# Four graph layers in float32: moving one group of tail products, and projecting a 32-column tile in four column tiles

## The chip, the cores and the metric

The kernel runs on one core of one Trainium2 chip. The metric is the device time of one execution in microseconds; the time given for a kernel is the median of its runs. A core has TensorE (PE, matrix products; its weight loads are listed as PEld), VectorE (DVE), ScalarE (ACT), GpSimd (POOL) and SyncE (SP). POOL and SP here issue DMA transfers and do nearly no computing. Each engine works through its own instructions strictly in order: an instruction that waits holds all that stand behind it on that engine.

## What is computed

Four graph layers on 2708 nodes with 512 features, on one 2708 x 2708 adjacency matrix. Each layer normalizes, aggregates over the graph, projects, and adds to `x`. Layers 0 to 2 differ in scaling, bias and self loops; layer 3 has a gated graph convolution beside an attention over the edges:

```python
h = relu(layernorm(x)); x = x + relu(aug @ h @ W0)            # layer 0, aug = D^-1/2 (A + I) D^-1/2
h = relu(layernorm(x)); x = x + (a_norm @ h @ W1.T + b1)      # layer 1
h = relu(layernorm(x)); x = x + relu(A_norm @ h @ W2)         # layer 2, with self loops
h = relu(layernorm(x))                                        # layer 3
x_a = attn @ (h @ W_sa); x_b = adj @ (h @ W_gcnb) + b_gcnb
x = x + sigmoid(attn_a * x_a + attn_b * x_b)                  # gates from type sums and h
```

## The kernel before

**Tiles.** The nodes are cut into four quarters of 677. Each quarter gives five tiles of 128 nodes (`KT = 5`, 20 in all), and 37 nodes are left over. Their first 32, of all four quarters together, make tile 20 (`NF`). The last 5 of each quarter, padded to 8, make 4 x 8 = 32 nodes for tile 21 (`NF + 1`); its 32 columns are repeated four times to fill 128 partitions. A matrix column block of one quarter is handled in two pieces (`U = 2`) of 339 columns.

**Aggregation.** The product of the 20 full tiles with the adjacency matrix is done by a two-level seven-product scheme: `OUTER` lists seven outer products, and each is done, for each piece `u`, by seven inner products of five accumulating matmuls (`product`, L506). `inner_x` and `inner_y` (L454, L471) build the sums of operands on DVE: `inner_y` makes `t1`, `t2`, `t4` and `t3` (L480 to L484), of 1695 elements a partition each; `add_loops` (L425, L431) adds multiples of the identity. `multiply` (L515) issues the inner products in a fixed order into banks `pa`, `pb`, `pa`, `pc`, `pd`, `pc`, `pd`; between them ScalarE copies `pa` (L543), DVE forms `u2` and `u3` (L549, L556), and `give` (L521, L525 to L534) adds results into `agg`. All of these and the tail products below take banks in turn from a pool of five PSUM buffers (`ps_agg`), with two more in `ps_out`.

**Tail products.** What tiles 20 and 21 contribute is added by `tail_products` (L567): for a quarter `q` and a piece, four matmuls with tile 20's 128 rows (L571), then four with 32 rows of tile 21 each, on the four row groups of the array (L576). `tails` (L603) runs them for a list of quarters and adds the four banks to `agg` (L621). `tail_rows` (L580) loads the rows they multiply and adds the self loops to them (L600).

**Layer 0 around the change.** `first_aggregate` (L662) is written out by hand because it also builds the degrees, and operand sums are kept for later layers in DRAM. Buffers are tight there: the tail rows of quarter 1 go into `own_t3`, which held `t3` of the products before, so they can be loaded only after product four's second piece has read it. The order is: product four's last piece, the tail products of quarters 0 and 1 (L849), then product five in two pieces (L857 to L864). Product five's second piece multiplies blocks `t1[1]`, which come by a load (L708) and an accumulating DMA (L712). `tc.issue_after(ins)` puts what it encloses behind `ins` on the engine of `ins`; where nothing says so, a scheduler decides the order of instructions on each engine when the program is built. `at_end` is the list of the additions into `agg` so far.

**The projection.** After the aggregation of a half, each tile's four column blocks of `agg` (`tile_cols`, L163) are the stationary operands of four matmuls, accumulated in one bank, with a weight matrix moving (`project`, L877, used in `next_x`; layer 3's gates in `gated`, L1016, with 257 columns; the attention's output in `attention`, L1114, with 512 or 256). For the tail tiles `tile_cols` gathers the columns into a scratch row by four copies (L174); for tile 21 `repeat` (L157, L160) doubles them twice to 128. Scratch rows come from `new_y`, which hands out two places in turn.

Of the kernel before, what the change touches and what calls it, by code (L numbers as in the profile page):

```python
# [8 lines left out]
FP = mybir.dt.float32  # L9
# [3 lines left out]
P = 128  # L13
D = 512
NC = D // P
N = 2708
NQ = 4
# [4 lines left out]
U = 2  # L22
W = (Q + 1) // U
NF = NQ * KT
NT = NF + 2
R1P = 8
G = NQ * R1P
# [10 lines left out]
def gnn_kernel(  # L38
# [20 lines left out]
    nc = tc.nc  # L59

    const = ctx.enter_context(tc.tile_pool(name="const", bufs=1))
# [11 lines left out]

    ident = const.tile([P, P], FP, name="ident")
    make_identity(nc, ident)
    again_ident = const.tile([P, G], FP, name="again_ident")
    nc.vector.tensor_add(again_ident, ident[:, 0:G], ident[:, G : 2 * G])
    for k in range(2, P // G):
        nc.vector.tensor_add(again_ident, again_ident, ident[:, k * G : (k + 1) * G])
    ones = const.tile([P, P], FP, name="ones")  # L80
    nc.vector.memset(ones, 1.0)
    first = const.tile([P, 32], FP, name="first")
# [43 lines left out]
    own_t3 = block(ends, 3 * BLK)  # L126
# [18 lines left out]
    def new_y():  # L145
        return take(y_places)
# [10 lines left out]
    def repeat(g, n):  # L157

        while n < P:
            nc.vector.tensor_copy(g[..., n : 2 * n], g[..., 0:n])  # L160
            n *= 2

    def tile_cols(a, t):  # L163

        cs = [a[:, f, :, c] for f in range(a.shape[1]) for c in range(a.shape[3])]
        if t < NF:
            q = t // KT
            return [full_cols(c[:, q // 2, q % 2], t) for c in cs]
        o, m = (KT * P, R0) if t == NF else (KT * P + R0 - PAD, R1P)
        if a.shape[5] == R0 + R1:  # L170
            o -= KT * P
        g = new_y().rearrange("p (c n) -> p c n", c=NC)
        for c, src in enumerate(cs):
            nc.vector.tensor_copy(  # L174
                g[:, c, 0 : NQ * m].rearrange("p (i q r) -> p i q r", i=2, q=2),
                src[:, :, :, o : o + m],
            )
        repeat(g[:, 0 : len(cs)], NQ * m)
        return [g[:, c] for c in range(len(cs))]


    def small_cols(tag, n):
# [320 lines left out]
    def bank(name):  # L503
        return ps_agg.tile([P, W], FP, tag="agg", name=name)
# [75 lines left out]
    def tail_rows(self_loops, q, pieces=None):  # L580


        blk = None
        if pieces is None:
            blk = free.pop(0)
            both = blk[:, 0 : 2 * U].rearrange("p (s u) w -> p s u w", s=2)
            pieces = [both[:, :, u] for u in range(U)]
            for s in range(2):
                nc.sync.dma_start(both[:, s], yt[s, :, q])
        else:  # L590
            for u in range(U):
                load_tails(q, u, pieces[u])
        if self_loops:
            o = (KT * P) % W
            for s, i, c0, n in (
                (0, ident[:, q * R0 : (q + 1) * R0], o, R0),
                (1, again_ident[:, q * R1P + PAD : (q + 1) * R1P], o + R0, R1),
            ):
                d = pieces[U - 1][:, s, c0 : c0 + n]
                nc.vector.tensor_add(d, d, i)  # L600
        return blk, pieces
# [60 lines left out]
    def first_aggregate(epilogue):  # L662
# [180 lines left out]
                    )  # L843
        for k, y in ((0, y22[0]), (1, y22[1]), (2, y22[0]), (3, y22[1])):
            minus_y22 = third_less(k, y, at_y[-1])
        own = own_t3[:, 0 : 2 * U].rearrange("p (s u) w -> p s u w", s=2)
        with tc.issue_after(minus_y22):
            rows = [early_rows, tail_rows(True, 1, [own[:, :, u] for u in range(U)])]
        tails(True, (0, 1), rows)  # L849
        t1 = [t2u, [y22[0], more[2], y22[1], t4[3]]]  # L850
        assert not free
        came = accumulated({QUAD[k]: t1[1][k] for k in (1, 0, 2, 3)}, "y12", 1, "y11")
# [4 lines left out]
        for u in range(U):  # L857
            more_loops = OUTER[5][2] - (OUTER[6][2] if u == 0 else 0)
            with tc.issue_after(came) if u == 1 else nullcontext():
                keep_all(t1[u], "t1", u, QUAD[1:3])  # L860
            with tc.issue_after(minus_y22 if u == 0 else at_end[-3]):
                ys = inner_y(t1[u], u, more_loops)
            keep_all(t1[u], "t1", u, QUAD[::3])
            multiply(xs_, ys, u, p5)  # L864
        with tc.issue_after(at_y[-1]):
            nc.vector.tensor_add(XC, XC, XA)
        free += t2u + [f for f in t1[1] if f is not more[2]]
# [7 lines left out]


    def project(w_sb, t):  # L877
        cs = tile_cols(agg, t)
        po = ps_out.tile([P, D], FP, tag="out", name="po")
        for c in range(NC):  # L880
            nc.tensor.matmul(  # L881
                po, cs[c], w_sb[:, c, :], start=(c == 0), stop=(c == NC - 1)
            )
        return po, cs

    def load_x(t, src):
        xt = take(xt_places)
# [3 lines left out]
    def next_x(ts, w_sb, scale, bias, src, colscale, after=None):  # L891
        for g in groups(ts):
            n, t0 = len(g), g[0]
            mv = small.tile([P, KT, 2], FP, tag="mv", name="mv")
            xts = []
            for s, t in enumerate(g):
                xt = load_x(t, src)
                po, _ = project(w_sb, t)
                y = new_y()
                if bias is None:  # L900
                    nc.scalar.activation(y, po, AF.Relu, scale=scale[:, t : t + 1])
                else:
                    nc.vector.scalar_tensor_tensor(
                        y, po, scale[:, t : t + 1], bias, ALU.mult, ALU.add
                    )
                nc.vector.tensor_add(xt, xt, y)  # L906
                nc.gpsimd.dma_start(xs[t], xt)  # L907
                stats(xt, mv[:, s, :])
                xts.append(xt)
            rstd = rstd_of(mv, n)  # L910
            if colscale is not None:
                nc.vector.tensor_mul(rstd[:, :n], rstd[:, :n], colscale[:, t0 : t0 + n])
            sh = shift_of(mv, rstd, n)
            for s, t in enumerate(g):
                normalized(t, xts[s], rstd[:, s : s + 1], sh[:, s : s + 1])
                if after is not None:
                    after(t)
# [5 lines left out]
    w_sb = []  # L923
# [92 lines left out]
    def gated(ts):  # L1016

        for t in ts:
            cs = tile_cols(agg, t)
            po = []  # L1020
            for k in range(2):
                pk = ps_out.tile([P, GW], FP, tag="out", name="pg")
                for c in range(NC):
                    nc.tensor.matmul(  # L1024
                        pk, cs[c], wg_sb[:, c, k, :], start=(c == 0), stop=(c == NC - 1)
                    )

                nc.scalar.activation(
                    ga[:, t, k : k + 1], pk[:, D // 2 :], AF.Tanh,
                    bias=hd[:, t, 2 + k : 3 + k], scale=0.5,  # L1030
                )
                po.append(pk)
            nc.vector.tensor_scalar(ga[:, t, :], ga[:, t, :], 0.5, 0.5, ALU.mult, ALU.add)
            y = new_y()
            for k in range(2):
                f = slice(k * (D // 2), (k + 1) * (D // 2))
                nc.vector.tensor_add(y[:, f], po[k][:, 0 : D // 2], bg_bc[:, f])
            nc.scalar.activation(y, y, AF.Copy, scale=ga[:, t, 1:2])
            nc.gpsimd.dma_start(xbs[t], y)
# [74 lines left out]
    def attention(t, columns, pieces=1):  # L1114
        xt = load_x(t, xs)
        y = load_x(t, xbs)
        nc.scalar.activation(xt, xt, AF.Copy, bias=0.5)
        sm = ps_sm.tile([P, NT], FP, tag="sm", name="pse")
        nc.tensor.matmul(sm[:, 0:1], columns(t), ones[:, 0:1], start=True, stop=True)
        cs = tile_cols(agg, t)  # L1120
        g = small.tile([P, 1], FP, tag="ge", name="ge")
        nc.vector.tensor_add(g, sm[:, 0:1], eps[:, t : t + 1])
        nc.vector.reciprocal(g, g)
        nc.vector.tensor_mul(g, g, ga[:, t, 0:1])
        n = D // pieces
        for k in range(pieces):
            f = slice(k * n, (k + 1) * n)
            pE = ps_out.tile([P, n], FP, tag="out", name="pE")
            for c in range(NC):
                nc.tensor.matmul(pE, cs[c], wsa_sb[:, c, f], start=(c == 0), stop=(c == NC - 1))  # L1130
            nc.vector.scalar_tensor_tensor(y[:, f], pE, g, y[:, f], ALU.mult, ALU.add)
            nc.scalar.activation(y[:, f], y[:, f], AF.Tanh, scale=0.5)
            nc.vector.scalar_tensor_tensor(xt[:, f], y[:, f], 0.5, xt[:, f], ALU.mult, ALU.add)
            for o, m, to in place(t):
                nc.gpsimd.dma_start(out[to : to + m, f], xt[o : o + m, f])
# [77 lines left out]
    xt_places = [a[:, k * D : (k + 1) * D] for a in flat for k in range(3)]  # L1213
    todo = [(t, lambda t, se_t=se_t: full_cols(se_t, t)) for t, se_t in todo]
    for k, t in ((1, NF + 1), (3, NF)):
        todo.insert(k, (t, lambda t: tile_cols(tail_sums, t)[0]))
    for n, (t, columns) in enumerate(todo):
        attention(t, columns, 1 if n + 1 < len(todo) else 2)

# [60 lines left out]
```

## Time and profile before

| | us |
|---|---|
| median of three runs | 2114.19 (2109.82 to 2119.08) |
| the profiled execution's own time | 2109.49 |
| its span, first to last instruction | 2107.3 |
| PE busy | 2059.4 (98%) |
| DVE busy | 1414.6 (67%) |
| ACT busy | 406.8 (19%) |
| POOL busy | 182.8 (9%) |
| projection matmuls L881, with columns from `agg` | 207.6, 480 records |
| mean granted clock of PE | 0.995 of full |

One float32 matmul appears as two records. In a group's line the first number is busy time, the second the mean duration of one record; records overlap, so a record's duration is more than its share of the time. In a timeline, a line gives start, length, engine, line of the kernel, operation, output and input; in brackets stands the idle time of the engine before it, and what ended it. In a list of waits the numbers are total, times and longest, in us. In a table by windows the columns are length, busy time of the engine, its records, the clock granted to PE, the busy share of the DMA engines, and GB/s.

### The profile page before, as it was taken

The numbers are of one execution on the slowest core, as the hardware profiler recorded it, in microseconds if no ns is written. First come the engines' busy times: TensorE is split into PE (matmuls) and PEld (weight loads), VectorE is DVE, ScalarE is ACT, GpSimd is POOL, SyncE is SP. The second block draws the span as 40 slices with busy tenths as digits, with TensorE's granted clock in tenths as the row PEclk, the third lists the DMA queues.
The fourth block names the chain that finished last, engine by engine and source line by source line (L and its number), as shares of the span: only waits on it lengthen the run. The fifth ranks groups of instructions, "written<-read, shape, count | busy, mean of one in ns | idle before, by whom it ended". The sixth has DMA issues, their size and how long they took to land.

```text
span 2107.3 us, 20074 instructions
## 1 busy us (share of the span) xinstructions
PE 2059.4 (98%) x7328; PEld 1284.3 (61%) x7328; DVE 1414.6 (67%) x2488; ACT 406.8 (19%) x827; POOL 182.8 (9%) x330
## 2 busy tenths in 40 slices
PE   5999989999999999999999999999999999999998
PEld 2666645646666555666664556666777666666665
DVE  4588867756777778766687889867537755666512
ACT  1430001130000011100002120000107533444410
POOL 0110111120000012100002120000001000000011
PEclk9999989999999999999999999999999999999999
DMA  9998594555545454655444574555451233233220
GB/s 369 300 376 272 186 314 157 192 179 180 176 159 174 138 178 138 230 170 172 165 157 161 201 240 161 182 165 171 161 177 61 93 103 112 86 103 101 90 73 26
DMA packets 79746, 360.86 MB, mean 171 GB/s; under 512 B 10668, under 2 KB 15660, under 8 KB 79520
## 3 DMA queue, kind: packets, MB, share of 16 engines
q1 hardware_dynamic: 50672, 245.43, 34.0%
q0 software_dynamic: 28976, 114.15, 16.7%
q8 instruction: 58, 0.95, 0.2%
q14 instruction: 40, 0.33, 0.0%
HBM read 294.61 MB, written 62.15 MB: 169 GB/s over the span
## 4 chain that ended last, share of the span: by engine, by line
PE 86%; DVE 6%; DMA 4%; issue 2%; POOL 1%; ACT 0%; SPq 0%; POOLq 0%; DVEq 0%; ACTq 0%
PE pe L1183 17%; PE pa L509 14%; PE pc L509 13%; PE pd L509 13%; PE po L881 9%; PE pb L509 7%; PE pE L1130 4%; PE pg L1024 3%; PE pt L571 3%; DMA obuf<-in_yb_dram 2%; PE pt L576 1%; PE pe L571 1%; DMA ends<-in_yt_dram 1%; DMA ends<-xs 1%; DVE ends L976 1%
## 5 line engine op out<-in xcount | busy, mean ns | idle before, releaser
L1183 PE MATMUL pe<-obuf,h 128*128 128x339 f32 x1280 | 372.8, 448 | 0.0
L509 PE MATMUL pa<-obuf,h 128*128 128x339 f32 x1040 | 315.8, 448 | 2.5 <-ACT h L223 1.4
L1183 PEld LDWEIGHTS pe<-obuf,h 128*128 128x128 f32 x1280 | 240.9, 189 | 126.6 <-issue 10.0
L509 PEld LDWEIGHTS pa<-obuf,h 128*128 128x128 f32 x1040 | 196.1, 189 | 106.3 <-issue 5.5
L881 PE MATMUL po<-ends,agg 128*128 128x512 f32 x480 | 207.6, 593 | 0.0
L1098 ACT ACTIVATE e<-r,nsr 128x339 f32<-128x339 f32 x352 | 170.8, 566 | 25.8 <-DVE obuf L1102 11.5
L509 PE MATMUL pc<-t,h 128*128 128x339 f32 x560 | 169.7, 449 | 2.7 <-DVE u L556 2.6
L509 PE MATMUL pb<-t,s 128*128 128x339 f32 x560 | 171.1, 452 | 1.1 <-DVE s L441 0.7
L509 PE MATMUL pd<-t,s 128*128 128x339 f32 x560 | 169.0, 448 | 0.0
L509 PE MATMUL pd<-obuf,s 128*128 128x339 f32 x550 | 166.3, 448 | 0.3 <-DVE agg L530 0.3
L543 ACT COPY v<-pa 128x339 f32<-128x339 f32 x56 | 24.7, 440 | 722.5 <-PE pa L509 719.4
L881 PEld LDWEIGHTS po<-ends,agg 128*128 128x128 f32 x480 | 90.9, 190 | 114.3 <-issue 109.3
L509 PEld LDWEIGHTS pc<-t,h 128*128 128x128 f32 x560 | 105.5, 189 | 58.7 <-DVE u L556 5.4
L509 PEld LDWEIGHTS pb<-t,s 128*128 128x128 f32 x560 | 106.4, 191 | 56.7 <-issue 1.8
L509 PEld LDWEIGHTS pd<-t,s 128*128 128x128 f32 x560 | 105.9, 189 | 54.1
L509 PEld LDWEIGHTS pd<-obuf,s 128*128 128x128 f32 x550 | 104.1, 189 | 53.8 <-DVE agg L530 1.3
L509 PE MATMUL pc<-obuf,s 128*128 128x339 f32 x450 | 136.1, 448 | 0.0
L509 PEld LDWEIGHTS pc<-obuf,s 128*128 128x128 f32 x450 | 85.1, 189 | 43.8 <-issue 0.5
L481 DVE TENSOR_TENSOR t<-obuf,t 128x1695 f32<-128x1695 f32 x55 | 105.5, 1918 | 0.0
L907 POOL DMA_DIRECT2D xs<-ends x66 | 35.9, 544 | 769.7 <-DVE ends L906 694.5
L1200 DVE COPY agg<-pe 128x339 f32<-128x339 f32 x16 | 7.5, 506 | 137.8 <-PE pe L576 137.8
L482 DVE TENSOR_TENSOR t<-obuf,t 128x1695 f32<-128x1695 f32 x52 | 99.7, 1916 | 0.1
(275 smaller groups left out, 2395.6 us busy)
## 6 DMA issues: line engine op xcount, KB each, us to landing
obuf<-in_yb_dram SPq DMA_DIRECT2D x132, 847.5 KB, 4.6
obuf<-osumt SPq DMA_DIRECT2D x100, 847.5 KB, 4.5
osumt<-obuf POOLq DMA_DIRECT2D x22, 847.5 KB, 10.3
xs<-ends POOLq DMA_DIRECT2D x66, 256.0 KB, 2.3
ends<-xs POOLq DMA_DIRECT2D x61, 256.0 KB, 3.9
obuf<-in_yt_dram SPq DMA_DIRECT2D x28, 339.0 KB, 3.6
obuf<-in_yb_dram POOLq DMA_DIRECT2D x11, 847.5 KB, 11.7
ends<-in_yb_dram SPq DMA_DIRECT2D x9, 847.5 KB, 9.0
```

The source lines that it names most:

```text
L481: nc.vector.tensor_add(t2, o22, t1)
L482: at_y.append(nc.vector.tensor_add(t4, o21, t2).ins)
L509: last = nc.tensor.matmul(ps, x[:, k, :], y[:, k, :], start=start and k == 0, stop=k == KT - 1, skip_group_check=not start,)
L543: at_v.append(nc.scalar.copy(v, pa).ins)
L571: nc.tensor.matmul(ps[c], h[:, NF, c * P : (c + 1) * P], tl[:, 0, :], start=start, stop=False)
L576: nc.tensor.matmul(ps[c], h[g, NF + 1, c * P : (c + 1) * P], tl[g, 1, :], start=False, stop=True)
L881: nc.tensor.matmul(po, cs[c], w_sb[:, c, :], start=(c == 0), stop=(c == NC - 1))
L907: nc.gpsimd.dma_start(xs[t], xt)
L1024: nc.tensor.matmul(pk, cs[c], wg_sb[:, c, k, :], start=(c == 0), stop=(c == NC - 1))
L1098: nc.scalar.activation(e[:, k], row, AF.Exp, bias=nsr[:, t, s : s + 1], scale=1.0)
L1130: nc.tensor.matmul(pE, cs[c], wsa_sb[:, c, f], start=(c == 0), stop=(c == NC - 1))
L1183: nc.tensor.matmul(pe[c], h[:, t, c * P : (c + 1) * P], a, start=(t == 0), stop=False)
```

## The change

Two edits. First, in layer 0 the tail products of quarter 1 are no longer run with those of quarter 0 ahead of product five, but between its first and second piece; the self loops on their rows are ordered behind the first piece's last `u3`. The loads of the rows carry no such order, since they are issued by SP and not by DVE. Second, for tile 21 the four column blocks are no longer repeated to 128 columns and accumulated: each 32-column block goes to a column group of its own in one bank, so the four partial results stand on the four partition groups; ScalarE copies the bank to a scratch row, and one matmul with `all_again` (128 x 128, one wherever row and column agree modulo 32) sums them and repeats the sum on all four groups. Only the attention's own column sums still use `repeat`.

```diff
-    again_ident = const.tile([P, G], FP, name="again_ident")
+    all_again = const.tile([P, P], FP, name="all_again")
+    again_ident = all_again[:, 0:G]
     nc.vector.tensor_add(again_ident, ident[:, 0:G], ident[:, G : 2 * G])
     for k in range(2, P // G):
         nc.vector.tensor_add(again_ident, again_ident, ident[:, k * G : (k + 1) * G])
+    for k in range(1, P // G):
+        nc.vector.tensor_copy(all_again[:, k * G : (k + 1) * G], again_ident)
...
-    def tile_cols(a, t):
+    def tile_cols(a, t, again=False):
...
-        repeat(g[:, 0 : len(cs)], NQ * m)
-        return [g[:, c] for c in range(len(cs))]
+        n = NQ * m
+        if again:
+            repeat(g[:, 0 : len(cs)], n)
+            n = P
+        return [g[:, c, 0:n] for c in range(len(cs))]
+
+    def tile_product(t, cs, ws):
+        n = ws[0].shape[-1]
+
+        def bank():
+            return ps_out.tile([P, n], FP, tag="out", name="po")
+
+        po = bank()
+        if t <= NF:
+            for c in range(NC):
+                nc.tensor.matmul(po, cs[c], ws[c], start=(c == 0), stop=(c == NC - 1))
+            return po
+        for c in range(NC):
+            nc.tensor.matmul(po[c * G : (c + 1) * G], cs[c], ws[c], start=True, stop=True)
+        y = new_y()[:, 0:n]
+        nc.scalar.copy(y, po)
+        po = bank()
+        nc.tensor.matmul(po, all_again, y, start=True, stop=True)
+        return po
...
-        own = own_t3[:, 0 : 2 * U].rearrange("p (s u) w -> p s u w", s=2)
-        with tc.issue_after(minus_y22):
-            rows = [early_rows, tail_rows(True, 1, [own[:, :, u] for u in range(U)])]
-        tails(True, (0, 1), rows)
+        tails(True, (0,), [early_rows])
...
             multiply(xs_, ys, u, p5)
+            if u == 0:
+                own = own_t3[:, 0 : 2 * U].rearrange("p (s u) w -> p s u w", s=2)
+                with tc.issue_after(at_u3[-1]):
+                    rows = tail_rows(True, 1, [own[:, :, v] for v in range(U)])
+                tails(True, (1,), [rows])
...
     def project(w_sb, t):
-        cs = tile_cols(agg, t)
-        po = ps_out.tile([P, D], FP, tag="out", name="po")
-        for c in range(NC):
-            nc.tensor.matmul(
-                po, cs[c], w_sb[:, c, :], start=(c == 0), stop=(c == NC - 1)
-            )
-        return po, cs
+        return tile_product(t, tile_cols(agg, t), [w_sb[:, c, :] for c in range(NC)])
```

`gated` and `attention` call `tile_product` in the same way in place of their own four matmuls.

## The prediction

> **What bounds the kernel now.** I read the page's busy table first, then the waits of TensorE, then the timeline around its longest wait inside the kernel, then the granted clock there. Busy time and waits of TensorE (PE):
>
> ```profile
> PE 2059.4 (98%) x7328; PEld 1284.3 (61%) x7328; DVE 1414.6 (67%) x2488; ACT 406.8 (19%) x827; POOL 182.8 (9%) x330
> ...
> PE dg_ps L292 <- DMA tails<-in_yt_dram: 16.8, 1, 16.8
> PE pt L571 <- DVE agg L530: 7.8, 1, 7.8
> ...
> PE pt L571 <- DVE agg L621: 2.1, 2, 1.6
> ```
>
> PE is the bound: 98% busy, and apart from the first load its one long wait is in layer 0's first tail products (L571). So a PE microsecond removed, or a PE wait removed, is a microsecond of the end, unless something else becomes late. The timeline there, PE and then VectorE (DVE):
>
> ```profile
> 268.87 0.84 PE L571 MATMUL pt<-tl,h 128*128 128x339 f32 x2
> 277.47 1.50 PE L571 MATMUL pt<-tl,h 128*128 128x339 f32 x2 [7.77 <-DVE agg L530]
> 280.61 2.63 PE L571 MATMUL pt<-tl,h 128*128 128x339 f32 x4 [1.64 <-DVE agg L621]
> ...
> 291.68 3.13 PE L509 MATMUL pa<-obuf,h 128*128 128x339 f32 x10
> ...
> 267.71 0.50 DVE L530 TENSOR_TENSOR agg<-pc,u 128x339 f32<-128x339 f32 x1
> 275.19 0.19 DVE L600 TENSOR_TENSOR ends<-ends,ident 128x32 f32<-128x32 f32 x1 [6.98 <-DMA ends<-in_yt_dram]
> ...
> 276.91 0.51 DVE L530 TENSOR_TENSOR agg<-pd,u 128x339 f32<-128x339 f32 x1
> ```
>
> The reader should see a head-of-line block. DVE stands at L600, which adds the self loops to the tail rows of quarter 1, until their DMA lands. Behind it waits L530, which would empty bank `pd`; PE's second tail matmul of the second half needs that bank. PE does not need quarter 1's rows yet. The clock, in windows of 3.413 us (columns: us, PE busy, granted clock, DMA share, GB/s):
>
> ```profile
> 268.68:272.09 3.41, 1.02 (x6) 1.00 1.03 416
> 272.09:275.50 3.41, 0.00 (x0) 0.50 1.04 364
> ...
> 282.33:285.74 3.41, 3.41 (x12) 0.50 1.07 227
> 285.74:289.16 3.42, 3.42 (x18) 1.00 1.03 212
> ```
>
> The wait also costs half clock from 272.1 to 285.7. DMA is full throughout.
>
> For the second edit I read 32-column matmuls (the column sums, L292) and one tail-tile projection (L881):
>
> ```profile
> 110.39:113.94 3.55, 3.55 (x48) 1.00 1.01 414
> 454.57:458.01 3.44, 3.44 (x10) 1.00 0.30 123
> ```
>
> 46 records (the window's count includes two neighbours) of 339 columns with 32-column weights take 3.55 us: a float32 matmul is two records, a full-width record takes 0.286 us (ten in 2.86), so 46 in a row would be 13.2. Four run side by side. Eight full 512-column records take 3.44.
>
> **What the Trainium skill says.** "TensorE: Matmul & The Clock Gate", Part 1, has the clock drop to half after an idle window and return after a busy one, in a free-running 3413 ns window; the trace fits, from 272.09 to 285.74 being four of them. "TensorEngine Tiling (Array Packing)", Key Properties: column tiles load and multiply in parallel, and a change of tiling mode drains the array. The trace agrees with both; entering costs about 0.1 us and leaving 0.1 (12 groups of 0.286 are 3.43 of the 3.55). "DMA: Bandwidth & Descriptors", Issuing engines are not separate DMA queues: loads from SP and POOL share the same 16 engines. Here they are at a share of 0.98 from 255 to 312 us.
>
> **The change, part by part.** Sums are against the profiled execution, 2109.49 us (span 2107.3), which is 4.7 below the median of 2114.19.
>
> Setup: three more 128x32 copies on DVE, 0.2 us each by L174's like, while PE waits 16.8 us for its first load: 0; exposed they would be 0.6.
>
> Layer 0's tails. L600 leaves this place. In the built order DVE now runs, after L530 of `pc` (to 268.1): six L431 pieces (five in 1.05 and one 0.24, about 1.15 pitched), L530 of `pd` to 269.7, L468 to 270.5, L480 to 272.3, the first two L621. PE: first tail matmul to 269.4, second 269.85 to 270.4, third when the first half's bank has been added, 272.9 (L621 still stands behind L480). So a gap of 2.5 us remains where 9.4 stood. The rest of this half: two full-array matmuls 1.14, the row-tiled set and switches 0.85: product five starts at 274.9 instead of 291.68, 16.8 earlier. Its `t2` is done at 275.0 and `t3` at 281.3, before `pb` (277.8) and `pc` (283.5) want them, so nothing there waits.
>
> Given back:
> - Quarter 1's products, 16 full and 16 row-tiled records, now stand behind the first piece: two halves of 2.38 + 0.78 and a switch, 6.4 us at full clock.
> - Eight L621 adds now stand on DVE ahead of piece two's L480. The piece is ordered behind the third-last add. From the tails' end: two adds 0.9, then two adds and the L431 pieces 2.2, L480 and L481 3.7, so `t2` is ready at +6.8. PE has the first product (held slightly by L431), 0.5 for ScalarE's copy, and four early matmuls of the second: done at +5.9. PE waits 0.9.
> - The 2.5 us gap: one window holds some 40% PE work. The 29% window above was throttled; so was 53.64 to 57.05, after one of 55%. I take one or two half-speed windows, 1.3 to 3.0 us, and, as phase may spare it, 1.5. Unthrottled, 0.
>
> Sum: -16.8 + 6.4 + 0.9 + 1.5 = -8.0.
>
> The moved loads. SP's last two 169.5 KB loads of these rows go behind one and three of the 847.5 KB loads for `t1` (L423). SP issued those by 268.7. The rows took up to 17.5 us to land, so expect 285 to 287; L600 now stands behind L556, at about 287, and delays PE only after 291. I count 0; 3 us later would cost 0, 8 us about 4. POOL's three x loads (L888, 293.0) now wait for quarter 1's later products, with the L419 writes of piece two behind them, which wait for L431 at about 303 anyway: 0. POOL's L419 at 276.88 goes 7 us earlier (its L431 no longer waits) and takes some 2 us of DMA from loads ahead of the accumulates.
>
> The tail tile (32 columns). Before: four matmuls, 3.44 (512) or 1.78 (257: half of 3.54). After: two rounds of the four tiles, 0.86, switches 0.2, one summing matmul 0.86: 1.92; at 257, 0.43 + 0.2 + 0.43 = 1.07. ScalarE's copy (0.63 by L1132; 0.36 at 257) lies between; two L160 copies (0.5) leave DVE.
> - Layer 0: two `pa` matmuls (1.14) cover the copy; the fourth tile waits 0.3 for its L174: -1.15.
> - Layer 1: the order puts a `pa` after three tiles, so a second round and switch cost 1.1: -0.4. Behind it the score vectors' L962, waiting for its DMA, moves ahead of L484 on DVE, and L556 follows later: +0.4, with -1 to +1.5 open.
> - Layer 2: split two and two: -0.6.
> - Layer 3's gates, two of 257: 1.4 less, 0.3 for ScalarE's exponentials ahead of the copy: -1.1.
> - Last attention tiles: the copy stands behind a tanh (ends at 2088.5); 3.44 becomes 2.9: -0.5.
>
> Sum -3.4, taken as -3.0; bounds -6.5 (all covered) and +1.
>
> Total -11.0: profiled about 2098.5; from the median, 2103.2.
>
> **Rivals.** A measurement of this kernel tells about 0.5% (10.6 us) from nothing.
> - *As above*, 0.60: 2103, own range 2099 to 2108.
> - *DMA takes the stall over*, 0.20. For: the share of 0.98, and L600 or the accumulates one order later. Against: 4 us of margin at the first, 6 at the second. A landing 8 us later than I expect gives 4 us back at L600 or at piece two: 2107.
> - *The tail tile pays nothing*, 0.10. ScalarE's copy and the second PSUM bank (two buffers) return 3 us at the six places: 2106. Against: matmuls of other products stand between in all but the last.
> - *Column tiles run in turn*, so the second edit doesn't do what it says, 0.04: four 512 places lose 1.1 each and two of 257 0.6, +5.6 instead of -3.0: 2111.8. The L292 rows speak against it.
> - *Slower*, 0.06: the accumulating DMA (L712) for piece two. Its last issue was at 283.13, median landing 12.1 us, so 295; piece two's L431 needs it at about 303. Each later microsecond is one lost; equal to before at a landing of 314, and 0.5% slower at 325: 2125. For it speaks only the full DMA.
>
> **How the numbers follow.** 2103 is the likeliest case. The range 2095 to 2112 takes that case's ends, both middle rivals, and 4 us for the spread of the runs shown (2109.8 to 2119.1); about 0.15 is outside. The edge for faster, 2103.6, cuts the first case: 0.46 of its 0.60 with chance in measurement, and 0.07 from the next two, are faster: 0.53. Slower 0.06, within 0.5% 0.41.
>
> **What would show it.** Right: product five's `pa` near 275 to 277 us, no L600 between L530 of `pc` and of `pd`, PE's waits on L530 gone and one on L621 near 2.5, the 16 tail matmuls after the first piece, its end (start of quarter 2's tails, 332.6 before) near 324.5; L881's like with four 32-column tiles in about 1.1 us. Wrong: a DMA wait of DVE at L600 beyond 291, or piece two's L431 waiting for the accumulates; half clock beyond 279; a PE wait on ScalarE ahead of the summing matmul; L556 late in layer 2's start.

## The result, and the profile after

The changed kernel takes 2097.6 us (median; 2094.3 to 2102.0) against 2112.8 us for the kernel before on the same chip: a ratio of 0.9926, 95% interval 0.9908 to 0.9945. That is 15.2 us less; the forecast was 2103, with a range of 2095 to 2112. The profiled execution took 2098.61 us (span 2096.7). Line numbers have shifted: L571, L576, L600, L621, L530, L509, L881 and L556 of before are L600, L605, L629, L650, L559, L538, L200 and L585 now; L203 is the 32-column tile, L205 ScalarE's copy, L207 the summing product.

The page's busy line of the changed kernel, and from the list of waits the longest waits of PE that are not on a DMA:

```profile
PE 2054.8 (98%) x7340; PEld 1279.6 (61%) x7340; DVE 1416.4 (68%) x2481; ACT 409.2 (20%) x833; POOL 182.8 (9%) x330
...
PE pt L600 <- DVE agg L650: 2.2, 2, 1.6
PE pc L538 <- DVE u L585: 2.1, 2, 1.8
```

The wait of 7.8 us on the emptying of `pd` is gone from the list. PE was and is 98% busy; its busy time is 4.6 us less, records at half clock counted at their longer time. The timeline of the changed kernel where the stall was, PE and then VectorE (start, duration, then the idle time before it and what ended it in brackets):

```profile
267.96 2.44 PE L600 MATMUL pt<-ends,h 128*128 128x339 f32 x8
...
274.13 1.41 PE L600 MATMUL pt<-tl,h 128*128 128x339 f32 x4 [1.60 <-DVE agg L650]
...
276.25 3.12 PE L538 MATMUL pa<-obuf,h 128*128 128x339 f32 x10
...
294.57 3.12 PE L538 MATMUL pd<-obuf,s 128*128 128x339 f32 x10 [0.91 <-DVE s L554]
...
325.65 2.45 PE L600 MATMUL pt<-obuf,h 128*128 128x339 f32 x8
269.05 0.50 DVE L559 TENSOR_TENSOR agg<-pc,u 128x339 f32<-128x339 f32 x1
...
270.58 0.51 DVE L559 TENSOR_TENSOR agg<-pd,u 128x339 f32<-128x339 f32 x1
...
293.93 0.17 DVE L629 TENSOR_TENSOR ends<-ends,all_again 128x5 f32<-128x5 f32 x1 [5.33 <-DMA ends<-in_yt_dram]
```

VectorE now empties `pd` 1.5 us after it started on `pc` (9.2 us before). One gap of 1.60 us is left on PE, and product five starts 8.29 us after quarter 0's first tail product, where it took 25.97 (7.1 us of these were quarter 1's tail products, which now come later). The self loops (L629) still wait for the rows, but at 288.6 and behind `u`, where PE loses 0.91 us to them in this execution. The clock in the window with most of the gap (us, PE busy, granted clock, DMA share, GB/s), on the grid of 3.41 us on which this execution's clock changes, as at 52.96 and 59.79:

```profile
271.41:274.83 3.42, 1.82 (x7) 1.00 1.03 421
```

No window at half clock follows the gap in this execution. The tail tile's product in layer 0, whole:

```profile
451.16 1.39 PE L203 MATMUL po<-ends 128*32 128x512 f32 x8
452.48 1.41 PE L538 MATMUL pa<-obuf,h 128*128 128x339 f32 x4
453.73 1.02 PE L207 MATMUL po<-ends,all_again 128*128 128x512 f32 x2
```

Eight records take 1.3 us to the start of the next group (3.44 before), two matmuls of `pa` cover ScalarE's copy, and the summing product takes 0.86.

**Where the time went, stage by stage.** From about 61 us on, PE's product starts can be laid side by side in all profiles. The table has, for each profiled execution, how much longer a stage was than in the first profile of before (us), from the starts of the same `pb` products; a negative number is a shorter stage, and the runs below are in it too. The stages left out are within 0.05 us everywhere, but for -0.25 between the start and layer 0's tails in the changed kernel's second profile.

| profile | start (to 61 us) | layer 0's tails (248 to 383) | layer 0's tail tile (383 to 464) | layer 1 (785 to 889) | layer 2 (1152 to 1297) | gates and attention (1297 to PE's last matmul) |
|---|---|---|---|---|---|---|
| before, again | +1.83 | +0.29 | 0.00 | +1.85 | +1.31 | +0.18 |
| move only | +1.55 | -9.01 | +0.04 | -0.18 | +0.25 | -0.01 |
| loops later | +0.14 | -8.12 | -0.01 | -0.01 | +0.04 | -0.06 |
| warm | -0.03 | +1.65 | +0.04 | +0.23 | -0.61 | +0.20 |
| tile only | -0.35 | +0.30 | -1.11 | -2.04 | -0.48 | -1.98 |
| changed | +1.75 | -8.70 | -1.12 | -0.78 | -0.12 | -1.75 |
| changed, again | -1.57 | -6.28 | -1.11 | -1.10 | -1.41 | -1.82 |
| rows early | +1.83 | -8.98 | -1.11 | -1.49 | +2.26 | -1.74 |
| rows and piece | +2.15 | -6.96 | -1.11 | -1.19 | -1.42 | -1.77 |
| adds first | +0.92 | -8.60 | -1.11 | -1.46 | -0.24 | -1.72 |
| serial tiles | +1.42 | -8.36 | +1.51 | +0.73 | +9.84 | +4.30 |

The start differs by up to 3.7 us between executions, whatever the kernel, and it goes with the clock: in the profiles that start 1.4 to 2.2 us later, two windows of 3.41 us ran at half clock before 61 us; in those between -0.35 and +0.92 one did; in the changed kernel's second profile none. Layers 1 and 2 move by 1.9 and 1.3 us between the two profiles of before, and layer 0's tails by 2.4 us between the two of the changed kernel. The tail tile's column and the last one repeat within 0.3 us among kernels with the same projection, so a step can be read from them that no whole time resolves.

### The profile page after: what moved, and what is told of

It is laid out like the page before. It is cut to its first block, busy times and chain, and to the rows that moved or that the text cites. A ratio compares the mean times of both kernels' runs of the same rounds, so it can differ in the third digit from the quotient of the medians.

```text
span 2096.7 us, 20100 instructions
## 1 busy us (share of the span) xinstructions
PE 2054.8 (98%) x7340; PEld 1279.6 (61%) x7340; DVE 1416.4 (68%) x2481; ACT 409.2 (20%) x833; POOL 182.8 (9%) x330
## 3 DMA queue, kind: packets, MB, share of 16 engines
q0 software_dynamic: 28976, 114.15, 16.8%
## 4 chain that ended last, share of the span: by engine, by line
PE 87%; DVE 6%; DMA 4%; issue 1%; ACT 1%; POOL 0%; SPq 0%; POOLq 0%; DVEq 0%; ACTq 0%
PE pe L1202 17%; PE po L200 15%; PE pc L538 14%; PE pd L538 14%; PE pa L538 13%; PE pb L538 7%; PE pt L600 3%; DMA obuf<-in_yb_dram 2%; DMA ends<-in_yt_dram 1%; PE pt L605 1%; PE pe L600 1%; DVE ends L1001 1%; DMA ends<-xs 1%; PE dg_ps L321 1%; DVE t L511 0%
## 5 line engine op out<-in xcount | busy, mean ns | idle before, releaser
L200 PE MATMUL po<-ends,agg 128*128 128x512 f32 (+2 forms) x968 | 352.1, 521 | 1.3 <-DVE ends L1058 1.0
L538 PE MATMUL pa<-obuf,h 128*128 128x339 f32 x1040 | 317.1, 449 | 2.5 <-ACT h L252 1.4
L200 PEld LDWEIGHTS po<-ends,agg 128*128 128x128 f32 x968 | 181.3, 190 | 154.3 <-issue 137.4
L538 PEld LDWEIGHTS pa<-obuf,h 128*128 128x128 f32 x1040 | 195.6, 190 | 110.0 <-issue 9.8
L538 PE MATMUL pb<-t,s 128*128 128x339 f32 x560 | 171.2, 452 | 1.8 <-DVE s L470 1.0
L538 PE MATMUL pc<-t,h 128*128 128x339 f32 x560 | 169.5, 448 | 2.1 <-DVE u L585 2.1
L538 PE MATMUL pd<-t,s 128*128 128x339 f32 x560 | 169.0, 448 | 0.0
L538 PE MATMUL pd<-obuf,s 128*128 128x339 f32 x550 | 166.5, 448 | 1.3 <-DVE s L554 0.9
L538 PEld LDWEIGHTS pb<-t,s 128*128 128x128 f32 x560 | 106.2, 190 | 57.2 <-DVE t L510 2.1
L538 PEld LDWEIGHTS pc<-t,h 128*128 128x128 f32 x560 | 105.7, 189 | 57.3 <-DVE u L585 3.6
L538 PEld LDWEIGHTS pd<-t,s 128*128 128x128 f32 x560 | 105.8, 189 | 54.1
L538 PEld LDWEIGHTS pd<-obuf,s 128*128 128x128 f32 x550 | 104.0, 189 | 55.2 <-DVE s L554 1.5
L538 PE MATMUL pc<-obuf,s 128*128 128x339 f32 x450 | 136.0, 448 | 0.0
L538 PEld LDWEIGHTS pc<-obuf,s 128*128 128x128 f32 x450 | 85.1, 189 | 43.8 <-issue 0.5
L510 DVE TENSOR_TENSOR t<-obuf,t 128x1695 f32<-128x1695 f32 x55 | 105.5, 1918 | 0.0
L578 DVE TENSOR_TENSOR u<-v,pb 128x339 f32<-128x339 f32 x56 | 28.4, 507 | 106.1 <-PE pb L538 106.0
```

Of the source, the lines that this page charges most:

```text
L200: nc.tensor.matmul(po, cs[c], ws[c], start=(c == 0), stop=(c == NC - 1))
L510: nc.vector.tensor_add(t2, o22, t1)
L538: last = nc.tensor.matmul(ps, x[:, k, :], y[:, k, :], start=start and k == 0, stop=k == KT - 1, skip_group_check=not start,)
L578: at_u2.append(nc.vector.tensor_add(u2, v, pb).ins)
```

## The experiments

**The move alone, and the projection alone.** The first takes over only the move of quarter 1's tail products:

```diff
...
-        tails(True, (0, 1), rows)
+        tails(True, (0,), [early_rows])
...
+            if u == 0:
...
+                with tc.issue_after(at_u3[-1]):
+                    rows = tail_rows(True, 1, [own[:, :, v] for v in range(U)])
+                tails(True, (1,), [rows])
```

The second takes over only `all_again`, `tile_product` and their callers:

```diff
+            nc.tensor.matmul(po[c * G : (c + 1) * G], cs[c], ws[c], start=True, stop=True)
...
+        nc.scalar.copy(y, po)
...
+        nc.tensor.matmul(po, all_again, y, start=True, stop=True)
```

> Only layer 0's second tail products are moved; the tail tile is projected as before. In the stretch from the start of quarter 0's tail products to the start of quarter 2's, my theory (VectorE no longer stands at quarter 1's self loops ahead of emptying bank pd) expects what the whole change showed there: 9.2 us less (66.9 to about 57.7), one gap of 1 to 2.5 us on PE where 9.4 us stood, and a median ratio of about 0.9957 (9 us of 2113). If the rest of what the medians gained beyond the profile (2.3 us) belongs to this edit, because the stall is mostly longer than in the one profiled execution of before, the median is 11 to 12 us lower, ratio 0.9945. The rival, that the four-tile projection brought most of the gain, expects 4 us or less here, ratio 0.998.

> Only the second tail tile's projection is changed; layer 0's tail products stay where they were. My theory: the 7.8 us wait of PE on emptying pd (9.4 us with the next one) and the half clock after it stay, the six places where the tile is projected give 3 to 4 us (in the profile of the whole change 3.8), ratio 0.9982 (0.9976 to 0.9988). The rival, that the projection carries what the medians gained beyond the profile, expects 6 us or more, ratio 0.997. That it pays nothing: ratio 1.000 within 0.0005.

Move only: 2102.1 us, ratio 0.9953 (0.9941 to 0.9966), 9.9 us less; stage -9.01. Tile only: 2105.1 us, ratio 0.9970 (0.9959 to 0.9982), 6.3 us less; its stall stands as it did:

```profile
277.11 1.50 PE L600 MATMUL pt<-tl,h 128*128 128x339 f32 x2 [7.27 <-DVE agg L559]
```

The product of the two ratios is 0.9923, the whole change's 0.9926: within the intervals, of about 0.001 each way and 0.002 for the whole, the parts add up, and nothing shows that one feeds the other. The move behaves as my theory says. The projection is worth more than my theory's 3 to 4 us: its median reaches the rival's number, and the four columns with the tile in them are 5.6 us shorter in this profile (5.1 over all profiles, below).

**Which half of the move counts.** In this kernel quarter 1's products stay where they were; only the two self-loop additions stand later on VectorE:

```diff
+        tails(True, (0,), [early_rows])
         own = own_t3[:, 0 : 2 * U].rearrange("p (s u) w -> p s u w", s=2)
-        with tc.issue_after(minus_y22):
-            rows = [early_rows, tail_rows(True, 1, [own[:, :, u] for u in range(U)])]
-        tails(True, (0, 1), rows)
+        with tc.issue_after(at_end[-4]):
+            rows = tail_rows(True, 1, [own[:, :, u] for u in range(U)])
+        tails(True, (1,), [rows])
```

> The kernel before, its tail products in their old place on PE; quarter 1's self loops are only put behind the first of the second half's additions of quarter 0 on VectorE. It tells what stalls: the place of the two small additions on VectorE, or the place of quarter 1's products on PE. If it is the additions, as I think: PE's wait on the emptying of pd is gone, product five's first matmul comes 5 to 8 us earlier relative to quarter 0's first tail product (26.0 us after it before, 18 to 21 now), some 3 us of waiting remain because the banks of quarter 0 are emptied behind t3's and t4's sums, ratio 0.9965 (0.996 to 0.9975). If the products have to stand behind the first piece to gain, because quarter 1's rows land too late whatever VectorE does: the wait only changes its name to the rows' DMA, and the time is within 1 us of before, ratio 0.9995 to 1.0005.

2104.3 us, ratio 0.9960 (0.9947 to 0.9974). Timeline of this kernel, PE and then VectorE:

```profile
266.76 2.44 PE L571 MATMUL pt<-ends,h 128*128 128x339 f32 x8
...
283.71 3.13 PE L509 MATMUL pa<-obuf,h 128*128 128x339 f32 x10
...
279.02 0.19 DVE L600 TENSOR_TENSOR ends<-ends,ident 128x32 f32<-128x32 f32 x1
```

Product five starts 16.95 us after quarter 0's first tail product, 9.0 earlier than before (expected 5 to 8), and the stage is 8.12 shorter, where the move gives 9.01. Two additions of 0.19 and 0.16 us in the wrong place on VectorE were the stall: by the time they are reached here (279.0) the rows are in, and they wait for nothing. PE's waits of 1.2 and 1.8 us that are left are on the additions of L621. What the place of quarter 1's products on PE is worth isn't resolved: the 0.9 us between the two profiles is less than the 2.7 us by which three profiles with the move differ in this stage (-6.28 to -9.01).

**Do the four tiles run side by side?** The changed kernel with all four 32-column products added up in one column group, so that they can't overlap; 32 rows are copied and summed:

```diff
-            nc.tensor.matmul(po[c * G : (c + 1) * G], cs[c], ws[c], start=True, stop=True)
+            nc.tensor.matmul(po[0:G], cs[c], ws[c], start=(c == 0), stop=(c == NC - 1))
...
-        nc.scalar.copy(y, po)
+        nc.scalar.copy(y[0:G], po[0:G])
...
-        nc.tensor.matmul(po, all_again, y, start=True, stop=True)
+        nc.tensor.matmul(po, all_again[0:G], y[0:G], start=True, stop=True)
```

> The changed kernel, but the second tail tile's four 32-column matmuls add up in one and the same 32-column group, so that they must run one after the other; ScalarE copies 32 rows, and the summing matmul has 32 rows of weights. If the four tiles run side by side in the changed kernel, as I think: a set of eight 512-wide records takes 3.4 us instead of 1.1 to 1.3, four such sets and two of 257 columns make 10 to 12 us more than the changed kernel, so about 2108 to 2110, ratio to before 0.9975 to 0.9985, the records 0.43 us apart. If they run in turn already: within 1 us of the changed kernel, ratio 0.9926.

2116.4 us, ratio 1.0023 (1.0016 to 1.0030): by the ratios about 20 us more than the changed kernel (the profiles' spans differ by 20.3), where 10 to 12 were expected. Layer 0's place costs 2.6 us more (1.51 against -1.11), as a serial set should: its eight records take 3.55 us to the next group's start, 1.32 in the changed kernel. So the tiles do overlap. The surplus is in layer 2, which is 10 us longer. PE, then ScalarE there:

```profile
1238.79 1.12 PE L207 MATMUL po<-ends,all_again 32*128 32x512 f32 x2 [1.87 <-ACT ends L205]
...
1263.08 4.82 PE L538 MATMUL pa<-obuf,h 128*128 128x339 f32 x10 [3.58 <-ACT v L572]
...
1237.64 0.63 ACT L1138 ACTIVATE ends<-ends 128x512 f32<-128x512 f32 x1 [5.72 <-DMA ends<-xs]
1238.18 0.56 ACT L205 COPY ends<-po 32x512 f32<-32x512 f32 x1
...
1262.07 0.63 ACT L1138 ACTIVATE ends<-ends 128x512 f32<-128x512 f32 x1 [9.21 <-DMA ends<-xs]
```

ScalarE stands at the 0.5 that it adds to an attention tile's x (L1138), whose load is still on its way; the copy for the summing product, and later that of `v`, stand behind it: the block that was taken off VectorE, on another engine. After each of the two waits ten records also take longer (4.53 and 4.82 us, 3.02 elsewhere): one window at half clock follows each. In the changed kernel's profile L1138 stands behind the copy, with a wait of 0.77 us, and PE waits for nothing there: the copy is free by the order on ScalarE. The scheduler made that order anew for this kernel, so this run's whole time is no measure of the overlap; layer 0's place is.

**The rows' load.** The load of quarter 1's rows put back where before had it, the two additions (now `tail_loops`) left behind the first piece:

```diff
...
+        rows = tail_rows(False, 1, [own[:, :, v] for v in range(U)])
         tails(True, (0,), [early_rows])
...
                 with tc.issue_after(at_u3[-1]):
-                    rows = tail_rows(True, 1, [own[:, :, v] for v in range(U)])
+                    tail_loops(1, rows[1])
```

and in the second kernel besides

```diff
-            with tc.issue_after(minus_y22 if u == 0 else at_end[-3]):
+            with tc.issue_after(minus_y22 if u == 0 else at_end[-5]):
```

> The changed kernel, but the load of quarter 1's rows is issued where the kernel before issued it, ahead of the loads of t1's blocks; the two self-loop additions and the products stay behind the first piece. If the 5.3 us that VectorE waited for these rows (and the 0.9 us that PE lost behind it, on s of L554) come from the load's new place in SP's queue: that wait is gone, PE's 0.9 us are gained, everything from quarter 1's products on is 0.9 us earlier than in the changed kernel. The rival: the two or three larger loads that now stand behind the rows make the accumulating loads of the second piece later, and PE waits there instead; then it is within 0.5 us of the changed kernel, or behind it.

> As the run before, and the second piece's sums are ordered behind quarter 1's first four additions instead of its last but two. If PE's two short waits at that piece (0.53 us on ScalarE's v, 0.39 us on t3 of L510) come from the order on VectorE alone: both gone, 1.8 us less than the changed kernel in all, median near 2095.5. If the piece waits for its accumulating loads anyway: the waits stay, and the time is that of the run before.

Rows early: 2096.0 us, ratio 0.9926 (0.9912 to 0.9939). The last of the rows lands at 279.1 and not at 293.9, and L629's wait and PE's 0.91 us are gone. But this loss isn't steady where the rows are loaded late, either: in "move only", in the changed kernel's second profile and in "adds first" (both below) they land at 291.4, 289.1 and 284.9, the self loops wait 2.12, 0.45 and 0 us, and PE loses nothing to them. In rows early PE waited 0.38 and 2.15 us in quarter 0's second half instead of 1.60, because a subtraction ahead of both `pc` and `pd` on VectorE waited 2.72 us for its own load (1.53 in the changed kernel). That wait is 3.40 in "adds first", whose loads are queued as in the changed one, so I can't put it down to the loads' order. Net -0.3 us in the stage: a tie. Rows and piece: 2100.4 us, ratio 0.9943 (0.9930 to 0.9955), and the stage is 2.0 us longer than in rows early: both small waits went, and one of 3.55 us came. PE at the second piece in rows early, then PE and VectorE in rows and piece:

```profile
307.55 2.55 PE L538 MATMUL pa<-obuf,h 128*128 128x339 f32 x8 [0.53 <-ACT v L572]
310.50 3.12 PE L538 MATMUL pb<-t,s 128*128 128x339 f32 x10 [0.39 <-DVE t L510]
...
310.55 3.12 PE L538 MATMUL pb<-t,s 128*128 128x339 f32 x10 [3.55 <-DVE t L510]
313.51 3.02 PE L538 MATMUL pa<-obuf,h 128*128 128x339 f32 x10
...
304.54 0.61 DVE L460 SCALAR_TENSOR_TENSOR obuf<-ident,obuf 128x45 f32<-128x45 f32 x3 [1.57 <-DMA obuf<-in_yb_dram]
305.07 1.92 DVE L509 TENSOR_TENSOR t<-ends,obuf 128x1695 f32<-128x1695 f32 x1
...
308.57 1.92 DVE L510 TENSOR_TENSOR t<-obuf,t 128x1695 f32<-128x1695 f32 x1
```

The piece's self loops (L460), put ahead of four additions, wait 1.57 us for the last accumulating load, which lands at 304.52. `t1` (L509) starts 1.5 us sooner than in rows early, but the four additions (1.75 us) now stand between it and `t2` (L510), the sum that PE's `pb` wants (the expectations call it `t3`). So `t2` starts where it did, at 308.57 (308.52 in rows early), and `pb` too. What is lost is on PE: in rows early eight records of the second `pa` product run ahead of `pb`, while `t2` is made; in this program all ten stand behind it, and eight records are 2.3 us. So the run doesn't decide between the two theories. It shows that the loads let the sums start 1.5 us sooner and no more; whether that would have paid with PE's old order is not shown.

**Does the half clock cost by itself?** Before, with twelve extra matmuls inside the stall, whose results nobody reads:

```diff
+                    if loaded and q == 0 and u == 1:
...
+                        for _ in range(12):
+                            nc.tensor.matmul(
+                                warm, h[:, NF, 0:P], pieces[0][:, 0, :], start=True, stop=True
+                            )
                     tail_products(ps, tl, True)
```

> The kernel before, with twelve matmuls of 339 columns added on PE between the two halves of quarter 0's tail products, whose results are used nowhere: 24 records, 6.9 us, inside the 7.8 us wait for pd. Nothing else is changed. They keep PE busy, so that the clock should not drop. If the half clock from 272.1 to 285.7 cost time by itself: the records after the wait run at 0.29 us instead of 0.57, and product five starts 1 to 3 us earlier (the emptying of the banks on VectorE holds the rest), ratio 0.9985 to 0.9995. If VectorE's additions set the pace there anyway: no gain, ratio 1.000, within 0.5 us in the profile.

2110.8 us, ratio 0.9997 (0.9988 to 1.0005); product five starts 27.2 us after the tails' start (25.97 and 26.44 in the two profiles of before). PE ran at full clock through the stall, but then waited 0.68 and 2.30 us for VectorE, and half clock followed from 280.0 to 286.9:

```profile
280.78 2.63 PE L571 MATMUL pt<-tl,h 128*128 128x339 f32 x4 [2.30 <-DVE agg L627]
```

Filling the stall bought nothing. It doesn't say what half clock costs alone, since half clock came back; it says that here PE follows VectorE's order.

**The last gap.** The changed kernel, the first piece's sums ordered behind quarter 0's first addition:

```diff
-            with tc.issue_after(minus_y22 if u == 0 else at_end[-3]):
+            with tc.issue_after(at_end[-8] if u == 0 else at_end[-3]):
```

> The changed kernel; the first piece's sums on VectorE are ordered behind the first addition of quarter 0's tails, so that the four additions of the first half stand ahead of the 1.9 us sum t1 (L509) and not behind it. If PE's last gap there (1.6 us before the third tail product of the second half) is the same kind of block, VectorE's order, it goes: product five's first matmul starts 1.3 to 1.7 us sooner after quarter 0's first tail product than the 8.3 us in the changed kernel. But t3 (L510) then ends some 2 us later, at about 11 us after the tails' start, and product five's second matmul wants it at 9.7: 1.0 to 1.5 us of that come back as a wait there, so 0 to 0.5 us are left in the stretch, and the median is that of the changed kernel within its uncertainty. If the rest of the gap were the clock or the banks and not VectorE's order, the gap stays and the second wait comes on top: 1 us slower.

2097.6 us, ratio 0.9930 (0.9910 to 0.9949). PE:

```profile
277.88 3.13 PE L538 MATMUL pb<-t,s 128*128 128x339 f32 x10 [1.63 <-DVE t L510]
...
285.28 3.13 PE L538 MATMUL pc<-obuf,s 128*128 128x339 f32 x10 [1.41 <-DVE obuf L513]
```

The gap was VectorE's order: it is gone, and product five starts 6.68 us after the tails' start, 1.6 sooner. It is given back at `t2` (L510; `t3` in the expectation), as expected, and once more at `t3` (L513), which now stands behind a 2.98 us addition; that I had not seen. VectorE has no slack in these 20 us, and its order only chooses where PE waits. None of these variants beats the changed kernel by more than can be measured.

**Both kernels once more.**

> The kernel before, profiled once more. The profiles so far stand 0 or about 1.7 us apart from about 60 us on, by whether one stretch of 3.4 us in the column sums ran at half clock; I take this to be chance, the same in every kernel. If so, this profile shows either the start of the first one (span near 2107.3) or one 1.5 to 1.8 us later (span near 2109), with the stall at quarter 0's tail products of the same 7 to 9.5 us. If instead the kernel before has a stall that varies by itself, the wait on pd differs by more than 1 us from the 7.8 us shown.

> The changed kernel, profiled once more. The stretch from quarter 0's first tail product to quarter 2's should again take 57 to 58.5 us with no wait on the emptying of pd; from about 60 us on the profile should stand either with the first profile of the changed kernel or about 1.7 us ahead of it (one stretch of 3.4 us at half clock in the column sums less); layer 1 with one wait on u3 (L585) where the kernel before mostly has two, layers 1 and 2 within 2 us of the first profile.

Before again: 2114.95 us, started 1.83 us later, with the same wait on `pd` (7.75 us). Changed again: 2095.78 us, started 1.57 us earlier than the first profile of before, more than I allowed for. Its tails took 60.5 us, not 57 to 58.5. PE, and then the windows of the clock in this execution:

```profile
271.06 2.63 PE L600 MATMUL pt<-tl,h 128*128 128x339 f32 x4 [2.14 <-DVE agg L650]
...
275.06 4.33 PE L538 MATMUL pa<-obuf,h 128*128 128x339 f32 x10
...
267.29:270.70 3.41, 1.55 (x4) 1.00 1.03 425
270.70:274.12 3.42, 3.06 (x8) 0.50 1.00 418
274.12:277.53 3.41, 3.41 (x13) 0.50 1.04 413
```

Here the gap of 2.14 us does bring two windows of half clock. Three groups are longer for it, by 1.2 (2.63 for 1.41), 0.7 (1.51 for 0.85) and 1.2 (4.33 for 3.12): 3.1 us. With them the rows are in time for PE; that and the longer gap account for the stage's -6.28 against -8.70.

## Why the prediction was right, point by point

- **Mechanism of the move: right.** The head-of-line block at the self loops was the stall; "loops later" shows it without moving a product.
- **Size of the move, -8.0: right on the mean, in part by luck.** Product five comes 17.7 us earlier (forecast 16.8; the gap is 1.6 us in this profile, not 2.5, and 2.1 to 2.8 us in "changed, again", "move only", "rows early" and "rows and piece"). From there to quarter 2's tails 8.5 us are given back (49.40 against 40.90): 6.4 for quarter 1's tails, exactly the forecast; 1.2 at the rows' load (the first piece is longer by this, with 0.91 of it as a wait), for which I counted 0; 0.9 at the second piece, as forecast. That is -9.2 between the first two profiles; the table's stage begins earlier and has -8.70, as PE lost 0.5 us ahead of the tails. The clock, 1.5, "as phase may spare it", was 0 in one execution and 3.1 in the next, where the rows' load cost nothing. Three profiles with the move (-8.70, -6.28, -9.01) average -8.0, but they spread over 2.7 us.
- **The moved load: late by 6 us, cheap.** I expected the rows at 285 to 287. They came at 293.9, in an execution that stands 1.75 us later from its start on, so at 292.1 on the prediction's scale. I had the issue right (the last at 270.1), and used the longest landing of before, 17.5 us; this one took 23.8. The limit that I named, 291, was passed by 1.1 us, and 1.2 us were lost.
- **The tail tile, -3.0: mis-sized.** Means of the profiles with the new projection (serial tiles left out) less those with the old: layer 0 -1.1 (forecast -1.15), layer 1 -1.7 (forecast 0; -1.4 without "before, again", which has a window at half clock there), layer 2 -0.4 (forecast -0.6, and lost in a spread of 3.7), gates and attention -1.9 (forecast -1.6). Together -5.1 (two slips in the forecast's terms don't matter: the switches around the L292 tiles are 0.12 us in all, not 0.1 each way, and layer 0's terms give -1.2); the median of tile only says 6.3, with 3.8 to 8.7 as its interval. The term that failed is layer 1's "+0.4 for L556 later". The profiles show the contrary: with the old projection PE mostly waited for `u` (L556) in two successive pieces, 1.9 to 2.3 us in all (once 2.44 us in the first alone); with the new one only in the first, 0.55 to 1.81. So the forecast's piece came out about even, and a wait in the next piece, which I hadn't counted, is gone. That piece in the first profile of before, PE and VectorE, then VectorE in the changed kernel:

```profile
879.96 3.13 PE L509 MATMUL pc<-t,h 128*128 128x339 f32 x10 [1.16 <-DVE u L556]
...
871.34 0.69 DVE L962 CUSTOM_DVE_ANT_0 ends<-ends 128x512 f32<-128x512 f32 x1 [4.76 <-DMA ends<-in_asa_dram]
...
856.20 0.69 DVE L987 CUSTOM_DVE_ANT_0 ends<-ends 128x512 f32<-128x512 f32 x1 [1.26 <-DMA ends<-in_asa_dram]
...
868.58 0.51 DVE L585 TENSOR_TENSOR u<-u,pc 128x339 f32<-128x339 f32 x1 [1.35 <-PE pc L538]
```

  Before, VectorE stands 4.76 us at the score vectors (L962, sums of weight products for the attention) until a load lands, with this piece's sums behind it, and the last of the eight stands between these sums. In the changed kernel's order that load is waited for 1.26 us, all eight (L987) are done before the piece's first `u`, and VectorE then waits for PE. That this order is the reason is read from the traces; I didn't test it.
- **Rivals.** DMA did take something over (1.2 us of PE in one profile, nothing in the others), not the stall. The projection pays; its tiles overlap. The accumulating load that I took for the way to slower was felt only where the piece was asked for sooner, 1.57 us on VectorE.
- **The total.** -8.0 and -5.1 are -13.1, inside the interval of the ratio (11.6 to 19.4 us). The remaining 2 us to the medians' 15.2 are within what the medians can tell; chance at the start (3.7 us) and in layers 1 and 2 suffices for them, and nothing else is shown. The median lies below the likeliest case's own range, 2099 to 2108. That the profiled execution took 2098.61, where I had "about 2098.5", is luck: it started 1.75 us late, which hid that in it each edit gained 0.7 to 0.8 us more than forecast.

## What to carry to other kernels

Where an engine works in strict order, look at what its waiting instruction holds up, not at what it waits for: moving 0.35 us of additions gave 8.1 us, about what the whole move gave (6.3 to 9.0). Before moving an operation to an idle engine, as the tile's copy to ScalarE, look in that engine's queue for operations that wait for loads, since they hold up what stands behind them (PE lost 1.87 and 3.58 us so in "serial tiles"). And compare profiles stage by stage, with a second profile of the same kernel for the spread: here the start and two layers vary by 3.7, 2.0 and 3.7 us among kernels that are alike there, about as much as the smaller edit is worth, while layer 0's tail tile and the last stage repeat within 0.3 us.

## What the runs showed of the hardware

- Gaps of the same length cost nothing or 3.1 us. In the changed kernel's second profile one of 2.14 us left a window with PE busy for 1.55 of 3.41 us, and two windows at half clock followed, the second of these after PE had been busy for 3.06 of 3.42. In "move only" and "rows and piece" one of 2.15 us was split between two windows (PE busy for 1.90 and 2.15, 1.96 and 2.71 us), and full clock followed; so it did in the changed kernel's first profile, after 1.82. "TensorE: Matmul & The Clock Gate", Part 1, a page of the Trainium skill, says that the window runs freely and is not reset by the kernel's start, and so varies from run to run; the profiles agree, with these windows' borders at 271.41, 270.70, 270.13 and 271.11 us. Its rule for the drop, one idle window, is stricter than what the second profile shows: PE was never idle there for a whole one.
- Landing times of the same 169.5 KB loads took at most 17.5 and 17.7 us in the two profiles of before. Issued behind larger loads of the same queue, the last of them took 23.8 and 21.9 us in the changed kernel's two profiles, 20.6 in "move only" and 24.0 in "serial tiles", but 15.0 in "adds first", with the DMA share near 1 in all; so its place in the queue alone doesn't set it.
- Four float32 32-column tiles of 512 columns take 1.32 us to the next group's start in layer 0 and 1.00 in the last attention tile, where one group in turn takes 3.55 in both ("serial tiles").
